# Layer 2's window attention: VectorE in a written order, the routing in set slots, the bias of the values and the experts' bias moved, the second norm from the first variance, the first expert weights asked for earlier

## The chip, the cores and the metric

The kernel runs on one core of a Trainium2 chip. The metric is the device time of one execution in microseconds. TensorE (PE) does the matmuls and transposes, VectorE (DVE), ScalarE (ACT) and GpSimd (POOL) the elementwise work, and SyncE (SP) issues most DMAs; each runs its own list of instructions in order and waits on semaphores for the others. All data are fp32.

## The reference

Four layers work on two images of 256 channels and 32 x 32 positions, that is 2048 tokens. Layers 0 and 1 are attentions over the images, layers 2 and 3 work on tokens. Layer 2, which the change touches:

```python
t = t + window_attention(layernorm(t))       # 8 heads of 32, windows of 64 tokens, shifted by 32
t = t + moe(layernorm(t))

def moe(x):                                  # 8 experts, two a token
    p = softmax(x @ Wr + br); top_p, top_i = top_k(p, 2); w = top_p / top_p.sum()
    xn = layernorm(x)                        # a second norm, on the norm's output
    y[e] = gelu((xn * ln_g[e] + ln_b[e]) @ W1[e] + b1[e]) @ W2[e] + b2[e]
    return sum(w[k] * y[top_i[k]] for k in range(2))
```

The window attention computes q, k and v from the normed tokens with a bias each, softmax(q k / sqrt(32) + relative position) v in each window, and a projection with the bias b_out. Layer 3 is an additive attention (tanh of all pairs of tokens in blocks of 1024) and another MoE.

## The kernel before, in words

Tokens are held as 16 tiles of 128 (`t`, 128 partitions x 16 x 256), eight tiles an image. Layers 0 and 1 take the span up to about 1640 us and are not touched. Then comes `window_attention` (L778), and at its end the generator of the routing is handed to `Late.run` (L1704), which plans the rest.

**The attention loop.** The first image is normed and transposed (`normed`, L824: 12 small VectorE instructions for the inverse root, 8 scales, 16 transposes, 4 copies). Six instructions or groups of them make one tile's way, spread over five rounds of a software pipeline (`for i in range(NT + 4)`): round i does `value(i)` (v, L898), `scores(i)` (q k, L871, then on VectorE L876 scale and bias, L882 maximum, L883 subtraction, on ScalarE L884 exp, on VectorE L885 sum and L886 reciprocal, on GpSimd L889 the two products that give the probabilities), `turn(i-2)` (transposes of the probabilities L908, copies L909 on ScalarE), a `project` of the next group of four tiles (q and k, L852, for the first 12 rounds), a step of the second image's `normed` (the first six rounds), `sums(i-3)` (L917, copy L925) and `output(i-4)` (L931; L935 adds b_out on VectorE into y; L936 adds y to t on GpSimd). From round 10 three pieces a round are taken of `late.dispatch(2, 0)`, the routing of the first image (in this code an image is a "b" of 8 tiles).

PE and ACT run the loop in the order in which it is written (`manual_schedule`); for DVE, POOL and SP a scheduler chooses the order.

**The routing (`Late.dispatch`, L1144).** For each half of four tiles, `gate` (L1127) norms the tokens (statistics L1087 and L1088, inverse root L1066 to L1079, scale L1097), transposes (L1108) and computes the router's logits (L1137). `route` (L1192) makes softmax, top two, the number of tokens of each expert, the slot of each token, the row of each weight tile and the shares. The second norm takes statistics of u again and scales it. Then 16 indirect DMAs on GpSimd (L1161, "the scatter") bring the tokens to their experts' slots in DRAM. At last `shift` (L1173) adds the experts' bias b2 to `t`, weighted by the shares: a transpose of the weights (ps_wT, L1179), matmuls (ps_b, L1187) and additions into `t`.

**The rest is planned by numbers.** In `Late.run` a dictionary gives each step a start and the distance of its pieces, in units of a made-up clock; `merge` interleaves the steps' pieces by it. D20 and D21 are the two images' dispatch, E20 and E21 the experts (each slot tile: xr read back by SP L1371, ps_x transposes L1379, ps_h L1404, gelu, ps_y L1424), C20 and C21 collect the results, A0 and A1 the additive attention (tanh L1622, ps_e L1631), and so on. Up to the start of E21 in the plan DVE, PE and ACT are scheduled, from there on they keep the written order. The experts' weights ("ew") are fetched tile by tile with indirect DMAs on GpSimd (L1322), into six buffers.

Of the kernel before, what the change touches and what calls it, by code (L numbers as in the profile page):

```python
# [19 lines left out]
F32 = mybir.dt.float32  # L20
I32 = mybir.dt.int32
U32 = mybir.dt.uint32
AF = mybir.ActivationFunctionType
# [4 lines left out]
P = 128  # L28
# [41 lines left out]
class Stack:  # L70
# [707 lines left out]
    def window_attention(self, t, late):  # L778
# [7 lines left out]
        with ExitStack() as ctx:  # L786
# [6 lines left out]
            w_qkv = self.load(w, "w_qkv", "(c p) o -> p c o", p=P)  # L793
            w_out = self.load(w, "wa_w_out", "(c p) o -> p c o", p=P)
            b_qk = self.load(w, "b_qk")
            b_v, b_out = self.load_row(w, "b_v"), self.load_row(w, "wa_b_out")


            rel = self.ins["rel_pos"]
# [19 lines left out]
            for x in probs:  # L819
                nc.gpsimd.memset(x, 0.0)  # L820

            uT, q, k, v, pT, o = {}, {}, {}, {}, {}, {}

            def normed(b):  # L824

# [19 lines left out]
            def project(g, part):  # L845

                if part == 0:
                    q[g], k[g] = (sb.tile([P, CC, CH], F32, name=n) for n in ("qh", "kh"))
                x, at = uT[g // 2], g % 2 * CH
                ps = late.misc([P, CH], "ps_qk")  # L850
                for c in range(CC):
                    nc.tensor.matmul(  # L852
                        ps, lhsT=w_qkv[:, c, part * P : (part + 1) * P], rhs=x[:, c, at : at + CH],
                        start=(c == 0), stop=(c == CC - 1),
                    )
                to = (q if part < CC else k)[g][:, part % CC, :]
                if part < CC:
                    nc.scalar.activation(to, ps, AF.Identity, bias=b_qk[:, part : part + 1])
                else:
                    nc.vector.tensor_scalar(to, ps, b_qk[:, part : part + 1], None, ALU.add)  # L860

            def scores(i):

                g, at = i // 4, (i % 4) * P
                s = p_s.tile([P, 4, CH], F32, name="ps_s")
                for o in range(CC):
                    for h in range(4):
                        rows = slice(D * h, D * (h + 1))
# [12 lines left out]
                m, rec = (self.small.tile([P, H], F32, name=f"wa_{n}") for n in ("m", "rec"))  # L881
                nc.vector.tensor_reduce(m, l, AX.X, ALU.max)  # L882
                nc.vector.tensor_tensor(l, l, broadcast(m, [P, H, WIN]), ALU.subtract)  # L883
                nc.scalar.activation(l, l, AF.Exp)  # L884
                nc.vector.tensor_reduce(m, l, AX.X, ALU.add)  # L885
                nc.vector.reciprocal(rec, m)  # L886
                for r in range(2):
                    rows = slice(WIN * r, WIN * (r + 1))
                    nc.gpsimd.tensor_tensor(  # L889
                        probs[i % RING][rows, :, rows], l[rows], broadcast(rec[rows], [WIN, H, WIN]), ALU.mult  # L890
                    )

            def value(i):
                x = uT[i // IT][:, :, i % IT * P : (i % IT + 1) * P]
                v[i] = sb.tile([P, C], F32, name="va", bufs=4)
                ps = late.misc([P, C], "ps_va")
                for c in range(CC):
                    nc.tensor.matmul(  # L898
                        ps, lhsT=x[:, c, :], rhs=w_qkv[:, c, 2 * C :], start=(c == 0), stop=(c == CC - 1)
                    )  # L900
                nc.vector.tensor_tensor(v[i], ps, b_v, ALU.add)

            def turn(i):
                pT[i] = sb.tile([P, H, P], F32, name="ptT")
# [22 lines left out]
            def output(i):  # L927
                x = o.pop(i)
                ps = late.misc([P, C], "ps_wo")
                for c in range(CC):  # L930
                    nc.tensor.matmul(  # L931
                        ps, lhsT=x[:, c, :], rhs=w_out[:, c, :], start=(c == 0), stop=(c == CC - 1)
                    )
                y = sb.tile([P, C], F32, name="y")
                nc.vector.tensor_tensor(y, ps, b_out, ALU.add)  # L935
                nc.gpsimd.tensor_tensor(t[:, i, :], t[:, i, :], y, ALU.add)  # L936

            for _ in normed(0):
                pass
            route, other = late.dispatch(2, 0), normed(1)  # L940
            engines = mybir.EngineType
            with tc.manual_schedule(engines={engines.PE, engines.Activation}):
                for part in range(2 * CC):
                    project(0, part)
                for i in range(NT + 4):
                    if i < NT:
                        value(i)
                        scores(i)
                    if 2 <= i < NT + 2:
                        turn(i - 2)  # L950
                    if i + 4 < NT:
                        project(i // 4 + 1, i % 4)
                    if i < 6:
                        next(other, None)
                    if 3 <= i < NT + 3:
                        sums(i - 3)
                    if 4 <= i:
                        output(i - 4)
                    if i >= 10:
                        for _ in range(3):  # L960
                            next(route, None)
            return route


# [25 lines left out]
class Late:  # L990
# [3 lines left out]
    def __init__(self, ctx, stack, t):  # L994
# [2 lines left out]
        nc, tc = self.nc, self.tc  # L997
        self.w = ctx.enter_context(tc.tile_pool(name="late_w", bufs=1))
        self.early = ctx.enter_context(tc.tile_pool(name="early_sb", bufs=2))
        self.made = {}  # L1000
        self.u, self.uT, self.logits, self.routes, self.affine, self.kT, self.qb = ({} for _ in range(7))

# [90 lines left out]
    def scale(self, dst, src, tiles, mv):  # L1093
        nc = self.nc
        rs = self.inverse_root(mv[:, :, 1], 1e-5)
        for k, i in enumerate(tiles):
            nc.vector.tensor_scalar(  # L1097
                dst(i), src(i), mv[:, k, 0:1], rs[:, k : k + 1], ALU.subtract, ALU.mult
            )
# [44 lines left out]
    def dispatch(self, *key, done=0):  # L1144

        l, b = key
        tokens = GROUPS[key]
        n = len(tokens)
        for half in range(done, n // 4):
            yield from self.gate(l, b, half)  # L1150
        yield from self.route(key, n)
        u = self.u[key]
        if l == 2:
            yield from self.norm(lambda i: u[:, i, :], lambda i: u[:, i, :], range(n))
        p, shares, slots, rows = self.routes[key]
        nc = self.nc

        before = []
        for i in range(n):
            for slot in slots:  # L1160
                ins = nc.gpsimd.indirect_dma_start(  # L1161
                    out=self.stack.slots_in[b % 2],
                    out_offset=bass.IndirectOffsetOnAxis(ap=slot[:, i : i + 1], axis=0),
                    in_=u[:, i, :], in_offset=None,
                ).ins
                for other in before:
                    self.tc.declare_no_dep(ins, other, reason="a slot takes one token")
                before.append(ins)
            yield None if l == 2 else 0.5
        if l == 2:  # L1170
            yield from self.shift(*key)

    def shift(self, *key):  # L1173

# [529 lines left out]
    def run(self, route):  # L1704
# [2 lines left out]
        self.sb = self.ctx.enter_context(self.tc.tile_pool(name="late_sb", bufs=2))  # L1707
        self.misc = lambda shape, name: p_m.tile(shape, F32, name=name, tag="ps_m")
        self.p_x, self.p_h, self.p_y, self.p_e = psum("lt_x", 1), psum("lt_h", 2), psum("lt_y", 1), psum("lt_e", 1)
        self.loaded = [  # L1710
            [self.sb.tile([P, WIDE], F32, name=f"ew{k}", bufs=LANES[2]) for k in range(2)] for _ in range(LANES[2])
        ]


        plan = {
            "D20": (route, (), -12, 0.86),
            "E20": (self.experts(2, 0, then=(2, 1)), ("D20",), 0, 2.4),
            "D21": (self.dispatch(2, 1), (), 5, 3.45),
            "E21": (self.experts(2, 1), ("D21", "E20"), 172, lambda now: 2.43 if now < 205 else 4.4),
            "C20": (self.collect(2, 0), ("E20",), 172, 2.0),  # L1720
            "A0": (self.additive(0), ("C20",), 211, 4.75),
            "N30": (self.gate(3, 0, 0), ("A0 half",), 420, 6.0),
            "C21": (self.collect(2, 1), ("E21",), 456, 2.0),
            "A1": (self.additive(1), ("C21", "A0 tanh"), 500, 4.6),
            "D30": (self.dispatch(3, 0, done=1), ("A0", "N30"), 515, 2.0),
            "E30": (self.experts(3, 0, then=(3, 1)), ("D30",), 600, 4.4),
# [110 lines left out]
```

## Time and profile before

| | us |
|---|---|
| median of 3 runs (lowest, highest) | 2885.95 (2885.02, 2887.11) |
| profiled execution | 2887.74 |
| its span, first to last instruction | 2886.0 |
| PE busy | 2635.3 (91%) |
| DVE, ACT, POOL busy | 1944.8, 1815.6, 1235.5 |
| mean granted clock of TensorE | 0.967 |
| first projection of layer 2 starts | 1640.51 |
| first scatter starts, last lands | 1779.64, 1803.88 |
| first expert matmul | 1810.59 |

The page gives busy time by engine, then the span in 40 slices with the busy share of each in tenths, the DMA queues, the chain of work that ended last, the costliest groups of instructions and the DMA issues. "Idle before" is idle time of an engine just ahead of an instruction, put down to what ended it. "L876" is a line of the kernel. In the order of time of one engine, a row has its start, its duration, the engine, the line, the operation, out<-in, and shapes as partitions x elements.

### The profile page before, as it was taken

The page shows a single profiled execution, that of the slowest core. Times are in us where ns is not written, and L with a number is a line of the kernel's source. Part 1 is how long each engine was busy: PE and PEld are TensorE (multiplying, and loading weights), DVE is VectorE, ACT ScalarE, POOL GpSimd, SP SyncE. Part 2 cuts the span into 40 slices and gives each one's busy share as a digit, 9 for nine tenths or more (in the row PEclk, how much of TensorE's full clock was granted, in tenths as well). Part 3 has the DMA queues.
Part 4 walks back from the last instruction along what each step waited for, and adds up shares of the span by engine and source line. Part 5 has one row for each costly group of instructions (what it writes and reads, how often), then busy time and mean ns, then how long its engine had stood idle before and what let it go on. Part 6 is the DMA issues. An engine that isn't in the chain of part 4 may idle for free. (4 is left out here: it accounts for less than half of the span.)

```text
span 2886.0 us, 77396 instructions
## 1 busy us (share of the span) xinstructions
PE 2635.3 (91%) x32006; PEld 1643.6 (57%) x32006; DVE 1944.8 (67%) x3642; ACT 1815.6 (63%) x2685; POOL 1235.5 (43%) x1302
## 2 busy tenths in 40 slices
PE   7899999999999998799999686999999988999987
PEld 3455555555555555555555454998666632465676
DVE  5999999999999999478789577633422343134242
ACT  2777777778777777255555231211699878889722
POOL 4877777777777775001111134244111112102242
PEclk9999999999999999899999897999999999899998
DMA  3000000000000000111010100543222001322354
GB/s 133 3 3 3 3 3 3 3 3 3 3 3 3 3 3 3 49 31 28 11 31 9 28 1 30 202 134 99 68 81 76 16 24 35 128 67 87 116 166 125
DMA packets 180577, 131.39 MB, mean 46 GB/s; under 512 B 130992, under 2 KB 162368, under 8 KB 173056
## 3 DMA queue, kind: packets, MB, share of 16 engines
q0 software_dynamic: 29232, 81.71, 8.5%
q1 hardware_dynamic: 147824, 44.25, 6.8%
q8 instruction: 251, 4.11, 0.6%
q10 hardware_dynamic: 3168, 0.48, 0.1%
q14 instruction: 102, 0.84, 0.1%
HBM read 181.24 MB, written 29.49 MB: 73 GB/s over the span
## 5 line engine op out<-in xcount | busy, mean ns | idle before, releaser
L188 ACT ACTIVATE sc<-sc,sa_shift 128x1024 f32<-128x1024 f32 x512 | 584.5, 1144 | 153.1 <-DMA sa_shift<-sa_min 150.8
L201 DVE STREAM_TRANSPOSE wt<-sc 128x1024 f32<-128x1024 f32 x512 | 601.5, 1207 | 0.2 <-ACT sc L188 0.2
L1622 ACT ACTIVATE th<-kT,qb 128x1024 f32<-128x1024 f32 x512 | 540.4, 1135 | 66.2 <-PE ps_e L1631 40.1
L211 PEld LDWEIGHTS ps_o<-wt,v 128*64 128x64 f32 x8192 | 444.4, 137 | 188.9 <-issue 106.2
L143 PE MATMUL ps_s<-kT,qT 64*32 64x512 f32 x8192 | 527.6, 595 | 18.0 <-ACT sc L153 17.2
L211 PE MATMUL ps_o<-wt,v 128*64 128x128 f32 x8192 | 505.0, 276 | 26.8 <-DVE oT L372 26.7
L166 POOL TENSOR_TENSOR fold<-sc 128x512 f32<-128x512 f32 x256 | 329.2, 1286 | 195.9 <-ACT sc L153 177.0
L168 POOL TENSOR_TENSOR fold<-sc,fold 128x512 f32<-128x512 f32 x256 | 328.4, 1283 | 21.4
L153 ACT COPY sc<-ps_s 128x1024 f32<-128x1024 f32 x256 | 256.0, 1000 | 111.0 <-PE ps_s L143 57.1
L1631 PE MATMUL ps_e<-th,pick 128*32 128x512 f32 x2048 | 305.7, 613 | 20.5 <-ACT th L1622 9.3
L1404 PEld LDWEIGHTS ps_h<-xe,ew 128*128 128x128 f32 x2320 | 278.1, 194 | 63.6 <-issue 39.0
L150 DVE TENSOR_SCALAR_CACHE_REDUCE sc<-ps_s 128x1024 f32<-128x1024 f32 x256 | 304.3, 1189 | 7.1 <-PE ps_s L143 6.6
L1404 PE MATMUL ps_h<-xe,ew 128*128 128x128 f32 x2320 | 295.0, 281 | 13.7 <-issue 5.6
L1424 PE MATMUL ps_y<-ew,h 128*128 128x256 f32 x1160 | 275.6, 387 | 8.2 <-ACT h L1410 5.6
L143 PEld LDWEIGHTS ps_s<-kT,qT 64*32 64x32 f32 x8192 | 134.4, 106 | 230.2 <-issue 163.4
L1424 PEld LDWEIGHTS ps_y<-ew,h 128*128 128x128 f32 x1160 | 215.6, 193 | 66.7 <-issue 23.0
L630 ACT ACTIVATE sc<-sc,l_least 128x1024 f32<-128x1024 f32 x128 | 146.7, 1147 | 125.8 <-DVE sc L617 125.5
L1415 DVE TENSOR_TENSOR hb<-ps_h,ew 128x512 f32<-128x512 f32 x115 | 79.4, 691 | 207.3 <-PE ps_h L1404 167.1
L1428 DVE COPY y<-ps_y 128x256 f32<-128x256 f32 x99 | 41.9, 423 | 229.7 <-PE ps_y L1424 209.9
L1393 ACT ACTIVATE h<-hb 128x512 f32<-128x512 f32 x115 | 71.5, 623 | 193.0 <-DVE hb L1415 173.7
L636 DVE STREAM_TRANSPOSE wt<-sc 128x1024 f32<-128x1024 f32 x128 | 153.3, 1225 | 46.0 <-ACT sc L630 25.4
L617 DVE TENSOR_SCALAR_CACHE_REDUCE sc<-ps_s 128x1024 f32<-128x1024 f32 x128 | 150.7, 1213 | 40.3 <-PE ps_s L609 40.2
(286 smaller groups left out, 3139.1 us busy)
## 6 DMA issues: line engine op xcount, KB each, us to landing
xr<-slots_in SPq DMA_DIRECT2D x99, 128.0 KB
slots_out<-y SPq DMA_DIRECT2D x99, 128.0 KB
sa_got<-sa_least SPq DMA_DIRECT2D x512, 0.5 KB
sa_shift<-sa_min SPq DMA_DIRECT2D x512, 0.2 KB
slots_in<-zero POOLq DMA_DIRECT2D x46, 128.0 KB
kh<-kh SPq DMA_DIRECT2D x32, 128.0 KB
qh<-qh SPq DMA_DIRECT2D x32, 128.0 KB
sa_sums<-sa_total SPq DMA_DIRECT2D x244, 1.0 KB
```

What stands on the lines that cost most here:

```text
L143: nc.tensor.matmul(ps[r][S * c : S * (c + 1), a, :].rearrange("p (b i) -> p b i", i=S), lhsT=qT[half, p, S * i : S * (i + 1)], rhs=keys[ha ...
L150: nc.vector.tensor_scalar(scores[m][0], flat[0], 1.0, None, ALU.mult, ALU.min, accum_out=least[m // 2][:, 0, h : h + 1])
L153: nc.scalar.copy(scores[m][1], flat[1])
L166: nc.gpsimd.tensor_tensor(y, a, b, ALU.subtract)
L168: nc.gpsimd.tensor_tensor(y, a, y, ALU.subtract)
L188: nc.scalar.activation(scores[m][r], scores[m][r], AF.Exp, bias=shift[m // 2][:, r : r + 1], scale=-1.0, accum_out=total[i][:, 2 * p + r, ...
L201: nc.vector.transpose(weights[i, h][:, 2 * p + r, :], x)
L211: nc.tensor.matmul(sums[i][64 * k : 64 * (k + 1)], lhsT=v[:, at % NT, 64 * (at // NT) : 64 * (at // NT + 1)], rhs=weights[i, h][:, :, S * ...
L1404: nc.tensor.matmul(ps[:, j, :], lhsT=a[:, c, at : at + P], rhs=x[:, c, :], start=(c == 0), stop=(c == CC - 1),)
L1424: nc.tensor.matmul(ps, lhsT=h[:, j, :], rhs=w2[:, j, :], start=(j == 0), stop=(j == HB - 1))
L1622: nc.scalar.activation(h, keys, AF.Tanh, bias=self.qb[b][:, s // G, g : g + 1])
L1631: nc.tensor.matmul(pe[i][c * U : (c + 1) * U, a, :], lhsT=self.pick[:, k, :], rhs=h[:, a, :], start=(k == 0), stop=(k == G - 1),)
```

## The change

Five parts, all of them in layer 2:

- VectorE joins PE and ACT in the written order of the loop, and the loop's body is cut differently for it: the softmax's sum, reciprocal and probabilities become `divide(i)`, after `sums(i-3)`. The 32 pieces of the routing are taken in numbers set round by round, half of them ahead of `output`, half behind.
- b_v no longer is added to the values. Since each row of probabilities sums to 1, it is put through the output projection once (`output_shift`, four matmuls with b_v spread over the columns) and added to b_out. b_out is added to `t` by GpSimd, tile by tile; `output` adds ps_wo to `t` on VectorE, in one instruction. The copies of v and the bias of k go to ScalarE.
- The variance after the first norm is var * rs * rs, so the second norm's statistics are not taken; its scaling goes to ScalarE, and the norm comes ahead of `route`. (The mean after the first norm is taken as zero.)
- `shift` leaves `dispatch` and becomes two steps of the plan, B20 at 100 and B21 at 215; C20 and C21 wait for them.
- The first expert weights (up and down of slot tile 0) are fetched before the scatter; the six weight buffers move to a pool that is there from the start.

```diff
-            b_v, b_out = self.load_row(w, "b_v"), self.load_row(w, "wa_b_out")
+            b_v, b_out = self.load(w, "b_v", "(c p) -> p c", p=P), self.load_row(w, "wa_b_out")
...
+            spread = w.tile([P, CC, P], F32, name="spread")
+            nc.gpsimd.tensor_copy(spread, broadcast(b_v, [P, CC, P]))
+
+            def output_shift():
+                ps = late.misc([P, C], "ps_wo")
+                for c in range(CC):
+                    nc.tensor.matmul(
+                        ps, lhsT=spread[:, c, :], rhs=w_out[:, c, :], start=(c == 0), stop=(c == CC - 1)
+                    )
+                nc.vector.tensor_tensor(b_out, b_out, ps, ALU.add)
...
-                if part < CC:
-                    nc.scalar.activation(to, ps, AF.Identity, bias=b_qk[:, part : part + 1])
-                else:
-                    nc.vector.tensor_scalar(to, ps, b_qk[:, part : part + 1], None, ALU.add)
+                nc.scalar.activation(to, ps, AF.Identity, bias=b_qk[:, part : part + 1])
...
                 nc.scalar.activation(l, l, AF.Exp)
+                weights[i] = l, m, rec
+
+            def divide(i):
+                l, m, rec = weights.pop(i)
                 nc.vector.tensor_reduce(m, l, AX.X, ALU.add)
...
-                nc.vector.tensor_tensor(v[i], ps, b_v, ALU.add)
+                nc.scalar.copy(v[i], ps)
...
-                y = sb.tile([P, C], F32, name="y")
-                nc.vector.tensor_tensor(y, ps, b_out, ALU.add)
-                nc.gpsimd.tensor_tensor(t[:, i, :], t[:, i, :], y, ALU.add)
+                nc.vector.tensor_tensor(t[:, i, :], t[:, i, :], ps, ALU.add)
...
-            with tc.manual_schedule(engines={engines.PE, engines.Activation}):
+            pieces = {8: 1, 9: 1, 10: 1, 11: 1, 12: 2, 13: 2, 14: 3, 15: 3, 16: 4, 17: 4, 18: 4, 19: 6}
+            with tc.manual_schedule(engines={engines.PE, engines.Activation, engines.DVE}):
                 for part in range(2 * CC):
                     project(0, part)
+                output_shift()
...
+                    if 2 <= i < NT + 2:
+                        nc.gpsimd.tensor_tensor(t[:, i - 2, :], t[:, i - 2, :], b_out, ALU.add)
                     if 3 <= i < NT + 3:
                         sums(i - 3)
+                    if i < NT:
+                        divide(i)
+                    for _ in range(pieces.get(i, 0) // 2):
+                        next(route, None)
                     if 4 <= i:
                         output(i - 4)
-                    if i >= 10:
-                        for _ in range(3):
-                            next(route, None)
+                    for _ in range((pieces.get(i, 0) + 1) // 2):
+                        next(route, None)
...
+            [self.w.tile([P, WIDE], F32, name=f"ew{run}{k}") for k in range(2)] for run in range(LANES[2])
...
         rs = self.inverse_root(mv[:, :, 1], 1e-5)
+        self.last_norm = mv, rs
...
+        again = self.early.tile([P, n], F32, name="again", bufs=1) if l == 2 else None
         for half in range(done, n // 4):
             yield from self.gate(l, b, half)
-        yield from self.route(key, n)
+            if l == 2:
+                mv, rs = self.last_norm
+                to = again[:, 4 * half : 4 * half + 4]
+                nc.vector.tensor_tensor(to, mv[:, :, 1], rs, ALU.mult)
+                nc.vector.tensor_tensor(to, to, rs, ALU.mult)
         u = self.u[key]
         if l == 2:
-            yield from self.norm(lambda i: u[:, i, :], lambda i: u[:, i, :], range(n))
+            rs = self.inverse_root(again, 1e-5)
+            yield 3.0
+            for i in range(n):
+                nc.scalar.activation(u[:, i, :], u[:, i, :], AF.Identity, scale=rs[:, i : i + 1])
+            yield 5.0
+        yield from self.route(key, n)
         p, shares, slots, rows = self.routes[key]
+        if key == (2, 0):
+            self.fetch(key, 0)
+            self.fetch(key, 0, 1)
...
-        if l == 2:
-            yield from self.shift(*key)
...
+            "B20": (self.shift(2, 0), ("D20",), 100, 5.0),
+            "B21": (self.shift(2, 1), ("D21",), 215, 6.0),
-            "C20": (self.collect(2, 0), ("E20",), 172, 2.0),
+            "C20": (self.collect(2, 0), ("E20", "B20"), 172, 2.0),
-            "C21": (self.collect(2, 1), ("E21",), 456, 2.0),
+            "C21": (self.collect(2, 1), ("E21", "B21"), 456, 2.0),
```

More of the change, by code (lines that the diff above doesn't have):

```diff
@@ L820, in window_attention @@
                 nc.gpsimd.memset(x, 0.0)
-            uT, q, k, v, pT, o = {}, {}, {}, {}, {}, {}
+            uT, q, k, v, pT, o, weights = {}, {}, {}, {}, {}, {}, {}
+            spread = w.tile([P, CC, P], F32, name="spread")
[7 more added lines that the diff above has]
+                nc.vector.tensor_tensor(b_out, b_out, ps, ALU.add)
             def normed(b):
@@ L999, in __init__ @@
         self.early = ctx.enter_context(tc.tile_pool(name="early_sb", bufs=2))
+        self.loaded = [
+            [self.w.tile([P, WIDE], F32, name=f"ew{run}{k}") for k in range(2)] for run in range(LANES[2])
+        ]
         self.made = {}
@@ L1148, in dispatch @@
         n = len(tokens)
+        nc = self.nc
+        again = self.early.tile([P, n], F32, name="again", bufs=1) if l == 2 else None
         for half in range(done, n // 4):
             yield from self.gate(l, b, half)
-        yield from self.route(key, n)
+            if l == 2:
[3 more added lines that the diff above has]
+                nc.vector.tensor_tensor(to, to, rs, ALU.mult)
         u = self.u[key]
         if l == 2:
-            yield from self.norm(lambda i: u[:, i, :], lambda i: u[:, i, :], range(n))
+            rs = self.inverse_root(again, 1e-5)
[4 more added lines that the diff above has]
+        yield from self.route(key, n)
         p, shares, slots, rows = self.routes[key]
-        nc = self.nc
+        if key == (2, 0):
+            self.fetch(key, 0)
+            self.fetch(key, 0, 1)
         before = []
@@ L1709, in run @@
         self.p_x, self.p_h, self.p_y, self.p_e = psum("lt_x", 1), psum("lt_h", 2), psum("lt_y", 1), psum("lt_e", 1)
-        self.loaded = [
-            [self.sb.tile([P, WIDE], F32, name=f"ew{k}", bufs=LANES[2]) for k in range(2)] for _ in range(LANES[2])
-        ]
         plan = {
```

## The prediction

> **What bounds the kernel now.** I read the rows of 40 slices first, then the stages in windows, then the chain and the waits of layer 2, then single engines in order of time. A slice is 72.15 us; layer 2's attention lies in slices 23 to 25.
>
> ```profile
> PE   7899999999999998799999686999999988999987
> DVE  5999999999999999478789577633422343134242
> POOL 4877777777777775001111134244111112102242
> ```
>
> TensorE is full nearly everywhere; it falls to 6 and 8 tenths just where VectorE and GpSimd rise. The windows show the same by stage: after the times come busy time of PE, weight load, DVE, ACT and POOL, then granted clock, DMA share and GB/s.
>
> ```profile
> 1680.00:1715.00 35.00, 26.66 (x298) 16.18 (x296) 26.00 (x65) 9.84 (x21) 11.25 (x12) 1.00 0.01 1
> 1752.00:1780.00 28.00, 18.73 (x203) 13.49 (x205) 26.06 (x98) 7.58 (x17) 8.80 (x10) 0.80 0.00 1
> 1780.00:1810.00 30.00, 15.68 (x76) 9.78 (x70) 13.68 (x58) 1.39 (x4) 23.90 (x26) 0.62 0.37 132
> 1810.00:1990.00 180.00, 179.66 (x1220) 167.12 (x1219) 84.27 (x248) 32.97 (x50) 62.11 (x62) 0.99 0.41 138
> 2045.00:2300.00 255.00, 254.91 (x1806) 164.66 (x1805) 67.77 (x151) 234.00 (x245) 30.90 (x31) 1.00 0.18 59
> ```
>
> So the attention loop (1650 to 1780) is bound by no single engine at first and by VectorE at its end (26.06 of 28), the scatter (1780 to 1810) by GpSimd, and the expert stages after it by TensorE. Up to the first expert matmul (ps_h, 1810.59) time saved in the loop counts in full, since what follows is serial: 16 scatters from 1779.64, the read-back xr issued at 1804.15, landed at 1808.64. The waits between 1640 and 1810 say what holds the loop:
>
> ```profile
> ACT l L884 <- DVE l L883: 59.8, 12, 6.7
> POOL probs L889 <- DVE wa_rec L886: 42.1, 6, 25.9
> DVE n_st L1087 <- POOL t L936: 11.3, 8, 3.4
> ```
>
> The last is the one on the path: VectorE's statistics wait 11.3 us in 8 waits for GpSimd's residual add, with the next softmax behind them. The starts of l (L876) give the period: 1650.76 for tile 0, 1679.94 for 5, 1702.93 for 8, 1735.97 for 12, 1771.75 for 15. Between 5 and 8 that is 7.66 us a tile, where TensorE's own pieces sum to 5.8 (value .96, scores .42, turn .95, project 1.88, sums .57, output .97).
>
> One resource more. VectorE's subtraction L883 takes 0.69 alone, and more beside GpSimd's probs:
>
> ```profile
> 1656.01 1.56 DVE L883 TENSOR_TENSOR l<-l,wa_m 128x512 f32<-128x512 f32 x1
> ...
> 1667.14 0.69 DVE L883 TENSOR_TENSOR l<-l,wa_m 128x512 f32<-128x512 f32 x1
> ```
>
> ```profile
> 1654.88 2.15 POOL L889 TENSOR_TENSOR probs<-l,wa_rec 64x512 f32<-64x512 f32 x2 [25.89 <-DVE wa_rec L886]
> ```
>
> The slow one begins with the second probs instruction (1656.0) and ends .54 after it (1657.03): it did its work when GpSimd was through. Maxima, bn_stats and reads from PSUM at such places keep their times. The scale into u (L1097) shows it too: four took 2.18 at 1741.61 against 1.45 alone (4 x .36).
>
> **The change part by part**, against the profiled execution (2887.74 us, span 2886.0, 1.7 around it; it lies 1.8 above the median 2885.95).
>
> 1. *Into the loop.* `output_shift` puts 4 matmuls of ps_wo's shape (.97) on TensorE between the projections and tile 0; with its start otherwise unmoved (it waits for w_qkv until 1640.51), l of tile 0 starts 1.0 later. b_v's load changes its queue and is used by nothing before that; I price it at nothing, since both loads are issued ahead of w_qkv's landing, and at some 2 us if it came after.
>
> 2. *The residual bias.* In the order as built, GpSimd's 16 adds of b_out (L936's shape, .73) don't stand in the loop's rounds: GpSimd is not in the hand-set order, and they are put in two blocks of 8, ahead of probs 0 and between probs 0 and probs 1. The second 8 each wait for VectorE's scale of the same tile for image 1, which stands in VectorE's order between the subtraction and the sum of tile 1. VectorE must finish 8 scales (2.9 alone), and each next scale meets the add that the last one released. Bounds: 0 if they pass each other, 8 x .73 = 5.8 if each waits; the first block can hold up the subtraction of tile 0 and some of the 12 small root instructions, 0 to 1.5; and tiles 2 to 4, in a chain of exp, turn, transposes and copies, up to 1.7 more. The row nearest is L1097's .73 lost under one GpSimd instruction, so I go towards the upper end: tile 5 starts 6 us later than now (1686), bounds 1.7 (with the 1.0 of part 1) and 10.
>
> The Trainium skill ("SBUF — State Buffer", "Who interferes with whom") has the rule: the pair of ports shared by VectorE and GpSimd is locked for a whole instruction, and the other engine fully blocks. It speaks against this change, and the L883 row agrees. The page excepts a VectorE instruction with one SBUF operand unless it is in a 2-port mode; L1097 has one tensor operand and was slow here. Under the rule the scales cost 5.8, under its exception 0.
>
> 3. *The loop, tiles 5 to 12.* kh's 8 bias adds (.75) and the 16 value copies (.42) go to ScalarE, which is busy 9.84 of 35 there: 12.6 us off VectorE, hidden on ScalarE, whose copies then lie ahead of exp by .4 each. The wait of L1087 on GpSimd goes, because the residual sum is VectorE's own (.42, in place of y). VectorE per tile: l .67, max .72, subtract .72, wait for exp .76, sum .69, reciprocal .2, residual .42 = 4.2. Late next is TensorE: 5.8 + .4 for what remains of waits = 6.2, so tiles 5 to 8 take 18.55 where they took 22.99. From tile 8 route pieces are added: four statistics pairs (.56) 6.4; root 2.4 and four scales 1.45 and 1.4 of stalls 9.45; two copies of uT with their transposes 6.75; router (1.69 on TensorE) 7.55: 30.15 for 33.04. Sum -7.3.
>
> 4. *Tiles 12 to 15.* The second norm loses 8 bn_stats and 8 aggregates (4.5) and 8 scales (4.1) on VectorE and gains four small instructions (.8); ScalarE does the scaling (hidden, 7.58 of 28 busy). VectorE in its written order: 4.2 + .4 + 2.2 + 2.4 + 1.45 + 1.3 of stalls = 11.97; 8.8 with two copies and the second router; 9.65 with the second root. 30.4 for 35.78: -5.4.
>
> 5. *Tile 15 to the first scatter.* Today the route is mixed into the loop's end and the scatter starts 7.9 after l of tile 15. In the new slots softmax and first choice come at round 15, the rest at 16: 45 small instructions at .20 = 9.0, tile 15's own 4.2, 3.6 of stalls = 16.8: +8.9.
>
> Parts 2 to 5: first scatter at 1779.64 + 6 - 7.3 - 5.4 + 8.9 = 1781.8, **+2.2** (bounds -2.1 and +6.2; a further -5 if the stalls of parts 3 to 5 vanish).
>
> 6. *Scatter to first matmul.* Five residual adds leave GpSimd's scatter (2.55) and two fetches enter it (2 x 1.31): 0. The fetches lie before scatters 7 on, so the weights come earlier, but xr lands last today and still does.
>
> 7. *Moved matmuls.* In the built order image 1's second 8 transposes (1.04) and two routers (2 x 1.69) come before ps_x, in time when TensorE is idle (15.68 of 30); now they are in the stage where it is busy 179.66 of 180: **-4.4**. `shift` for image 0 takes the place of image 1's there: 0 (its old place, at clock .5, was hidden). Image 1's (2 x (.5+1+1) = 5.0) goes among ps_e, with TensorE at 254.91 of 255 but ScalarE also at 234: 0 if ScalarE's tanh sets the end, 5 if TensorE does; I take **+3**, nearer to the row of the fuller engine. Table loads (1.28 at 1815.5 and 1846.17) are beside TensorE's work: 0.
>
> Sum +2.2 - 4.4 + 3 = +0.8: 2888.5 beside this execution, 2886.8 beside the median. I write **2886.5**.
>
> **Rivals.** Faster: adds and scales pass each other (part 2 at its lower bound, -2.1) and the stalls of 3 to 5 go too (-5): -7.1 - 4.4 + 3 = -8.5, 2877.5. For it: bn_stats and PSUM reads show no stall, and TensorE has 8 us of slack in 1680 to 1715 for making up lag. Against it: L883 and L1097.
>
> Slower: the written order of VectorE keeps the lag. Everything behind a held-up scale (sum and reciprocal of tile 1, so probs 1, its turn, image 1's uT) waits with it; tile 5 is then 10 late, image 1's shift is paid in full (+5), and transposes and routers run at the clock of .65 (a router took 3.15 there for 1.69), 1.5 of it on the path twice: +6.2 - 4.4 + 5 + 3 = +9.8, 2896. It decides from a lag of 9 us at tile 5. For it: clock .62 in 1780 to 1810, .80 before. Against it: TensorE's margin in tiles 5 to 8.
>
> The change doesn't do what it says: the loop is in VectorE's order, but the adds aren't in it; that is in the forecast already. If the period stays 7.66 because ScalarE's added work delays exp, part 3 loses its 4.4 in tiles 5 to 8: 2891, within the forecast's own range.
>
> **How the numbers follow.** No change (own range 2881 to 2892): .40; faster: .33; slower: .27. 0.2% is 5.8 us, about what can be told from no change. Two in ten cut off evenly from the outer cases leave 2875 to 2897.
>
> **What would show it.** Starts of l: tile 5 near 1686 (1682 for the faster case, 1690 for the slower); a period of 6.2 from 5 to 8; GpSimd's adds in two blocks with scales stretched to about 1.0; first scatter at 1782 and, as now, 31 us from it to the first ps_h; 4.4 less between the first ps_h and the last ps_y of image 0; the tanh stage 3 longer. It is wrong if the scales stay at .36, if the period stays above 7, or if later stages, whose plan is by numbers, fall differently.

## The result, and the profile after

The changed kernel is slower: 2897.45 us, median of 8 runs (2892.46 to 2902.53), against 2885.25 for the kernel before (8 runs, 2879.55 to 2888.22); ratio 1.0047, 95% interval 1.0036 to 1.0059. The forecast was no change at 2886.5, the range ended at 2897.0. The profiled execution took 2902.53 us, the slowest of the eight; its span is 2900.8, 14.8 more than the span before, where the medians differ by 12.2.

The same three rows of 40 slices, of the changed kernel:

```profile
PE   7899999999999998799999686899999989899987
DVE  5999999999999998377788456343522343134242
POOL 4877777778777775011111333244111011102142
```

In slices 23 to 26 VectorE reads 4 5 6 3 where it read 5 7 7 6, so work has left it; TensorE reads 6 8 6 8 for 6 8 6 9, so its hole has not closed. The stages tell more. In the lines of the changed kernel L885 is the scale and bias of l (before: L876), L898 the softmax's sum (L885), L947 the residual (L935), L970 GpSimd's add of b_out, L1132 the copies of uT (L1109) and L1160 the router (L1137). Windows of the kernel before and after, cut at tile 0, tile 8, tile 15 (starts of l), first scatter and first ps_h; columns as in the windows above. Before:

```profile
1702.93:1771.75 68.82, 49.26 (x510) 34.28 (x509) 55.58 (x175) 14.35 (x31) 19.67 (x21) 0.84 0.00 1
1779.64:1810.59 30.95, 16.62 (x82) 10.56 (x81) 14.63 (x61) 1.75 (x4) 24.73 (x26) 0.62 0.38 136
```

After:

```profile
1652.11:1707.68 55.57, 45.20 (x482) 27.60 (x482) 36.24 (x66) 20.66 (x43) 27.75 (x31) 0.91 0.01 1
1707.68:1773.57 65.89, 51.81 (x520) 36.90 (x518) 42.70 (x120) 18.42 (x40) 14.75 (x15) 0.82 0.01 1
1773.57:1791.66 18.09, 13.59 (x106) 9.95 (x104) 14.69 (x76) 8.12 (x20) 2.08 (x2) 0.72 0.00 1
1791.66:1827.21 35.55, 12.11 (x51) 10.48 (x51) 18.72 (x87) 2.41 (x7) 21.92 (x22) 0.54 0.62 228
```

Between tiles 8 and 15 VectorE's work fell by 12.9 us (55.58 to 42.70), as the prediction had it leave; the stage got only 2.9 shorter. VectorE now stands idle 23.2 us there, where it stood 13.2. Its waits in that window of the changed kernel (total, times, longest):

```profile
DVE l L885 <- PE ps_s L880: 6.9, 4, 2.1
DVE wa_m L898 <- ACT l L893: 5.3, 7, 0.8
DVE t L947 <- PE ps_wo L944: 4.9, 5, 1.7
DVE rt_lg L1164 <- PE ps_router L1160: 4.1, 2, 2.8
```

In the kernel before the first two are not in the list of that window at all. What stands behind such a wait, from VectorE in order of time:

```profile
1714.62 0.18 DVE L1110 BATCH_NORM_AGGREGATE n_mv<-n_st 128x2 f32<-128x6 f32 x1
...
1717.59 0.69 DVE L898 TENSOR_REDUCE wa_m<-l 128x8 f32<-128x512 f32 x1 [0.76 <-ACT l L893]
1718.31 0.20 DVE L899 RECIPROCAL wa_rec<-wa_m 128x8 f32<-128x8 f32 x1
1719.25 0.42 DVE L947 TENSOR_TENSOR t<-t,ps_wo 128x256 f32<-128x256 f32 x1 [0.74 <-PE ps_wo L944]
1719.59 0.16 DVE L1094 TENSOR_SCALAR ir_x<-n_mv 128x4 f32<-128x4 f32 x1
```

The routing's inverse root (from L1094 on) has its input n_mv at 1714.80 and starts at 1719.59, behind two waits of .75 in which VectorE does nothing. The time of each stretch in the profiled executions, with the prediction's terms:

| stretch | before | after | difference | predicted |
|---|---|---|---|---|
| span's start to tile 5 | 1679.94 | 1688.54 | +8.6 | +6 |
| tile 5 to 12 | 56.03 | 53.70 | -2.3 | -7.3 |
| tile 12 to 15 | 35.78 | 31.33 | -4.4 | -5.4 |
| tile 15 to first scatter | 7.89 | 18.09 | +10.2 | +8.9 |
| first scatter to first ps_h | 30.95 | 35.55 | +4.6 | 0 |
| first ps_h to first tanh | 238.6 | 233.2 | -5.4 | -4.4 |
| first tanh to the end | 836.8 | 840.4 | +3.6 | +3 |
| sum | | | +14.8 | +0.8 |

The two blocks of GpSimd's adds are where the built order had them:

```profile
1651.25 5.98 POOL L970 TENSOR_TENSOR t<-t,sb_wa_b_out 128x256 f32<-128x256 f32 x8 [8.32 <-DVE sb_wa_b_out L834]
1659.86 2.15 POOL L902 TENSOR_TENSOR probs<-l,wa_rec 64x512 f32<-64x512 f32 x2 [2.63 <-DVE wa_rec L899]
1663.03 5.84 POOL L970 TENSOR_TENSOR t<-t,sb_wa_b_out 128x256 f32<-128x256 f32 x8 [1.02 <-DVE u L844]
```

And VectorE beside them:

```profile
1655.24 0.65 DVE L1095 TENSOR_SCALAR ir_half<-ir_x 128x8 int32<-128x8 int32 x1
...
1657.49 0.17 DVE L1101 SCALAR_TENSOR_TENSOR ir_y<-ir_a,ir_y 128x8 f32<-128x8 f32 x1
...
1662.49 5.11 DVE L844 TENSOR_SCALAR u<-t,tok_mv,ir_y 128x256 f32<-128x256 f32 x8
```

Four root instructions of .17 took about .65 until the first block ended at 1657.23, and the eight scales took 5.11 for 2.9. The last thing to see is the hand-over to the experts:

```profile
1808.88 0.16 DVE L1181 TENSOR_TENSOR again<-again,ir_y 128x4 f32<-128x4 f32 x1
...
1816.38 0.69 DVE L1132 COPY uT<-ps_tr 128x512 f32<-128x512 f32 x1 [7.35 <-remote]
...
1818.55 3.15 PE L1160 MATMUL ps_router<-sb_wr,uT 128*128 128x8 f32 x14 [0.82 <-DVE uT L1132]
...
1821.55 0.67 PE L1415 MATMUL ps_x<-ident,xr 128*128 128x128 f32 x2
1822.82 0.19 DVE L1164 TENSOR_TENSOR rt_lg<-ps_router,sb_br 128x32 f32<-128x32 f32 x1 [3.75 <-PE ps_x L1415]
...
1826.74 0.73 DVE L1419 TENSOR_SCALAR xe<-ps_x,rt_affine 128x128 f32<-128x128 f32 x2
1827.21 3.14 PE L1440 MATMUL ps_h<-xe,ew 128*128 128x128 f32 x13 [4.99 <-DVE xe L1419]
```

ps_x is through at 1822.2, but xe stands behind the second image's top two on VectorE, which waited for the router, which waited for a copy: 5.7 us from ps_x to ps_h where it was 1.5.

### The profile page after: what moved, and what is told of

It reads as the page before. It is cut to its first block, busy times and chain, and to the rows that moved or that the text cites. A ratio compares the mean times of both kernels' runs of the same rounds, so it can differ in the third digit from the quotient of the medians.

```text
span 2900.8 us, 77381 instructions
## 1 busy us (share of the span) xinstructions
PE 2646.8 (91%) x32010; PEld 1654.6 (57%) x32010; DVE 1927.4 (66%) x3579; ACT 1832.7 (63%) x2723; POOL 1236.6 (43%) x1303
## 5 line engine op out<-in xcount | busy, mean ns | idle before, releaser
L188 ACT ACTIVATE sc<-sc,sa_shift 128x1024 f32<-128x1024 f32 x512 | 585.0, 1145 | 155.9 <-DMA sa_shift<-sa_min 155.8
L1440 PE MATMUL ps_h<-xe,ew 128*128 128x128 f32 x2320 | 295.8, 281 | 20.2 <-DVE xe L1423 7.8
L1460 PEld LDWEIGHTS ps_y<-ew,h 128*128 128x128 f32 x1160 | 216.8, 194 | 64.6 <-issue 20.9
```

The lines of the kernel that those rows point to most:

```text
L188: nc.scalar.activation(scores[m][r], scores[m][r], AF.Exp, bias=shift[m // 2][:, r : r + 1], scale=-1.0, accum_out=total[i][:, 2 * p + r, ...
L1440: nc.tensor.matmul(ps[:, j, :], lhsT=a[:, c, at : at + P], rhs=x[:, c, :], start=(c == 0), stop=(c == CC - 1),)
L1460: nc.tensor.matmul(ps, lhsT=h[:, j, :], rhs=w2[:, j, :], start=(j == 0), stop=(j == HB - 1))
```

## The experiments

Ratios are to the kernel before on the same chip, with 95% intervals. Times between stages are counted from tile 0's l, since that start moves by some 5 us between these profiles. Each of the five groups (e1 to e4, e5 to e8, e9 to e12, e13 to e16, e17 and e18) ran on a chip of its own. On three of these the kernel before takes 2881 to 2887 us, on the chips of e9 to e12 and of e17 and e18 2847 to 2848; there the stretches behind the first ps_h are shorter for every kernel profiled. So only ratios are compared between groups, and these not finely: the changed kernel has 1.0047 in the result and 1.0068 in e14, one other program 1.0006 in e10 and .9991 in e15. Differences under some 2 thousandths (6 us) are read within a group alone.

**The adds: e1 and e2.** The first leaves out the bias of the attention's output.

```diff
-                    if 2 <= i < NT + 2:
-                        nc.gpsimd.tensor_tensor(t[:, i - 2, :], t[:, i - 2, :], b_out, ALU.add)
```

> The changed kernel without GpSimd's 16 adds of b_out to t (so the attention's output bias is left out of the result). Theory A, the adds: they hold up VectorE's root, scales and the first softmaxes, and all of the 8.6 us by which tile 5 is late come from them and from the 1 us of output_shift; without them tile 5 starts at about 1682, the first scatter at 1784 and the time is about 2890 (ratio to the kernel before 1.002). Theory B, VectorE's written order: tile 5 comes early, but the rounds from 8 on, where route pieces stand between the softmax steps, give it back; first scatter 1788 or later, time 2894 to 2897. Theory C, the second image's routing ahead of the first xe: the distance from ps_x to the first ps_h stays at 5.7 us in either case.

Ratio 1.0042 (1.0028 to 1.0056), 2893.8 us. Tile 5 at 32.1 us after tile 0 (after 36.4, before 29.2), first scatter at 133.7 (139.6, 128.9). So the adds cost 4.3 at tile 5 and 5.8 at the scatter in these profiles: more than half of tile 5's lag of 7.2 is theirs. How much of it the time keeps lies between nothing (1.0047 in the result) and 7.5 us (2901.3 for e3 below, on the same chip, which reaches the first ps_h as late as the changed kernel, 175.1 us after tile 0). The greater part of the slowdown is there without the adds.

e2 also puts back the old residual (y on VectorE, t + y on GpSimd).

> The changed kernel with the residual as before (VectorE adds b_out to ps_wo into y, GpSimd adds y to t); all else as changed. Theory A: the block of adds is gone, so tile 5 at 1682; but statistics wait again for GpSimd's add (.73 plus .2) in rounds 6 to 14; first scatter 1786 to 1790, time about 2893. Theory B: first scatter at 1790 or later, time 2896 to 2900, since VectorE's order with the new wait is worse.

Ratio 1.0043 (1.0027 to 1.0059), 2897.1 us. Tile 5 at 32.5, first scatter at 138.0. It is not the wait for GpSimd's add that makes the difference to e1: between tiles 5 and 15 none is in VectorE's list of waits, and behind tile 15 there is one, of .5 us. First scatter to ps_h takes 32.7, and the long wait of the uT copy isn't there.

**The second image's start: e3.** `"D21": (..., 5, 3.45)` becomes `25`.

> The changed kernel with the second image's dispatch planned at 25 where it was 5, so that the first xe no longer stands behind its routing in VectorE's order. Theory C: ps_x to first ps_h is 1.5 us for 5.7, but the transposes and routers (4.4) are again in the expert stage, where TensorE is full: net -4.1 + 4.4, about 2897 to 2898. If instead the 4.1 was not on the path, the time rises to about 2901. Theories A and B expect nothing of it.

Ratio 1.0071 (1.0054 to 1.0088). ps_x to first ps_h still takes 6.0: up to the start of E21 the scheduler orders TensorE and VectorE, and it moved the second image's ready work ahead of the waiting experts all the same. The edit didn't make the difference it was meant to make; it says nothing for or against theory C.

**VectorE's order: e4, e5, e6.** e4 takes VectorE out of the written order of the loop.

```diff
-            with tc.manual_schedule(engines={engines.PE, engines.Activation, engines.DVE}):
+            with tc.manual_schedule(engines={engines.PE, engines.Activation}):
```

> The changed kernel with VectorE out of the written order of the loop (the scheduler orders it, as before); GpSimd's order as built then has all 16 adds ahead of the first probabilities. Theory B: rounds 8 to 15 get faster, from 65.9 us between tiles 8 and 15 to about 60, and the first scatter comes within 10 us of tile 15 for 18; time about 2888 in spite of the adds. Theory A: the probabilities of tile 0 start 3 us later still (11.7 us of adds ahead of them), and time is 2898 to 2902.

Ratio 1.0004 (0.9994 to 1.0013), 2884.8 us: nearly the whole loss is gone, with all 16 adds in a block ahead of the first probabilities. Tiles 8 to 15 take 51.2 us (after 65.9, before 68.8). Its window from tile 8 to 15:

```profile
1706.78:1757.99 51.21, 44.14 (x506) 31.54 (x505) 37.85 (x108) 18.54 (x41) 13.08 (x13) 0.90 0.01 2
```

and VectorE's waits in it:

```profile
DVE rt_lg L1164 <- PE ps_router L1160: 4.1, 2, 2.8
DVE t L947 <- PE ps_wo L944: 3.8, 5, 0.9
DVE wa_m L898 <- ACT l L893: 2.3, 3, 0.8
DVE l L885 <- PE ps_s L880: 1.7, 3, 0.8
```

Idle time is 13.4 us, 23.2 in the written order. The window also holds 4.9 us less of VectorE's work, which comes behind tile 15: from there to the first scatter e4 takes 21.1 us for 18.1. In tiles 8 to 12 the work is the same (20.8 and 20.9 us), and there e4 takes 27.8 us for 34.6. The idle time fell where the written order had VectorE stand at the next instruction of its list: before the sum until exp is back (5.3 to 2.3), and before the next l until TensorE has scored (6.9 to 1.7). The route's small instructions that could have filled these holes stood behind.

TensorE's clock has a part in it. In tiles 8 to 12 its granted clock is .87 in the changed kernel and 1.00 in e4, and its work there takes 29.2 and 25.0 us (297 and 295 matmuls). In the changed kernel TensorE idles for 3.6 us from 1723.8 to 1727.4; in the 3 us from 1728.68 on the clock is .50, and tile 11's value and scores take 2.6 us (1730.94 to 1733.51) where tile 10's took 1.45. The same loop in e9 and e1 has a clock of .95 there and takes 32.4 and 32.6 us. So 4.6 us of the 6.8 between the two orders are there at nearly the full clock, and some 2 come with the low one. No run here holds the clock and changes the order alone.

The next two have the written order in rounds 0 to 7 only, and from round 8 on only; the loop is cut in two with one list of engines each.

> The changed kernel with VectorE in the written order only in rounds 0 to 7 and free from round 8 on, where the route pieces stand. Theory B1 (the order hurts where route pieces are cut into it): about the time of the kernel with a free VectorE, 2884 to 2887, tiles 8 to 15 in about 52 us and the first scatter about 129 us after tile 0. Theory B2 (it hurts from the first round): 2894 to 2897.

> The changed kernel with VectorE free in rounds 0 to 7 and in the written order from round 8 on. Theory B1: 2895 to 2899, tiles 8 to 15 in about 66 us. Theory B2: about 2886.

Ratios 1.0020 (1.0010 to 1.0031) and 1.0058 (1.0041 to 1.0075). Tiles 8 to 15 take 51.9 and 65.9 us, just as in the free and the written kernel, whatever came before them. Theory B1: the order hurts from round 8 on, where route pieces are cut into it. Between tiles 5 and 8, where none are, the written order takes 19.1 us and the free one 20.2. e5's ratio is not quite e4's, but the intervals overlap.

**The slots: e8.** Three pieces a round from round 10 on, as before, in the written order.

> The changed kernel with three route pieces a round from round 10 on, as before, VectorE in the written order. Theory D (the slots alone are wrong): 2888 to 2890, since the pieces end at round 19 with 30 taken and the second scales come earlier or later by at most a round. Theory B1 (any route piece in a written order costs the wait of the softmax beside it): 2895 to 2900.

Ratio 1.0054 (1.0037 to 1.0071). Tiles 8 to 12 take 38.7 us for 34.6, tile 15 to the first scatter 13.2 for 18.1; the scatter comes 5.9 sooner (133.6 after tile 0), but from it to the first ps_h it takes 38.8 for 35.6. The time is that of the changed kernel, as theory B1 has it: the set slots alone are not what slows it.

**The adds with a free VectorE: e7.** b_out goes into ps_wo by a matmul:

```diff
+                nc.tensor.matmul(ps, lhsT=late.ones[0:1, :], rhs=b_out[0:1, :], start=False, stop=True)
```

> The changed kernel with VectorE free and GpSimd's 16 adds taken out: b_out goes into ps_wo by a matmul of one row of ones with the row of b_out (16 more matmuls of 1 x 128 by 1 x 256). Theory A for what is left of the lag: tile 5 comes 31 us after tile 0 where it came 34.8 with a free VectorE and 36.4 in the changed kernel, and the time falls by about 4 to 2880 or 2881. If the adds don't matter once VectorE is free: 2885.

Ratio 1.0022 (1.0012 to 1.0032). Tile 5 comes at 29.7, the lag is gone as expected; the first scatter comes at 126.1 (e4 127.3), since the 16 more matmuls make the rounds longer (each has two rows in the trace, .69 us together; tiles 5 to 8 take 22.2 for 20.2). No gain.

**The hand-over: e9 and e10.** The plan's first part keeps the written order on TensorE and ScalarE, and the second image's dispatch starts at -30, so that its counts and its top two come behind the first experts. Both edits are in one run.

```diff
-        merge(plan["E21"][2])
         engines = mybir.EngineType
+        with self.tc.manual_schedule(engines={engines.PE, engines.Activation}):
+            merge(plan["E21"][2])
...
-            "D21": (self.dispatch(2, 1), (), 5, 3.45),
+            "D21": (self.dispatch(2, 1), (), -30, 3.45),
```

> The changed kernel with the first part of the plan in the written order on TensorE and ScalarE and the second image's dispatch planned from -30 on, so that its counts stand behind the first experts on TensorE and its top two behind the first xe on VectorE. Theory C: the first scatter to the first ps_h takes 31 to 32 us for 35.6, the first scatter stays at 140 us after tile 0, the time falls by about 4, ratio 1.003. If the lost 4 us come back in the expert stage (the routing that was in front has to go somewhere): ratio 1.0045 to 1.005.

> The changed kernel with VectorE free in the loop and the hand-over of the run before. If both causes are separate and add: first scatter 127 us after tile 0, first ps_h 31 to 32 us later for 38.4, time 6 below the kernel with a free VectorE alone, ratio 0.998. If the expert stage gives back what the hand-over gains: ratio 1.000.

The mechanism is as theory C has it: first scatter to ps_h 30.9 and 31.2 us for 35.6 and 38.4. The ratios don't show it: 1.0044 (1.0027 to 1.0062) and 1.0006 (0.9996 to 1.0015), while e10's first ps_h is at 155.9, 3.9 before that of the kernel before. But 4 us are 1.4 thousandths, less than the ratio of one program moves from chip to chip. What the time keeps of the 4.6 is not shown; in e10 there is no gain on the kernel before.

**Parts alone: e11 and e12**, in the kernel before.

> The kernel before with the second norm from the first variance alone (8 statistics, 8 aggregates and 8 scales off VectorE, four small instructions added, scaling on ScalarE); the norm stays behind the route. By part 4 of the prediction 7.8 us of VectorE's work go in a stage that it bounds: if that holds with a free order, the first scatter comes 4 to 8 us earlier and the time is 2878 to 2881 (ratio 0.998). If the scatter waits for the route's slots and not for u, nothing: 1.000.

> The kernel before with the experts' bias as two steps of the plan alone. By part 7: image 0's in the place of image 1's, image 1's 5.0 us of matmuls in the tanh stage, 0 to 5 of it on the path; ratio 1.000 to 1.002. If the emptier time before the first ps_x is filled with the second image's transposes and routers, 4.4 us come off the expert stage and the ratio is 0.9985 to 1.000.

The second norm alone: 1.0008 (0.9998 to 1.0018). Tile 15 comes 2.5 us earlier (118.5 for 121.0), the first scatter not (128.8). It doesn't wait for the route's slots, as the expectation's second case had it: these are there at 1777.8. ScalarE begins to scale u only at 1778.42, behind its copies, and GpSimd's residual add ends at 1779.41; the scatter starts at 1779.58. So the number came out by another wait. The bias as steps of the plan alone: 1.0016 (1.0005 to 1.0026), first ps_h at 159.1, so whatever it costs lies behind.

**Where the earlier start goes: e13 to e18.** First the kernels before and after once more, with e10's kernel and its variant with b_out on TensorE, on one chip.

> The kernel before once more, with a profile from the chip of the three runs beside it, so that stages can be set side by side. Ratio 1.000 within .001; tile 0 to the first ps_h 159 to 161 us.

> The changed kernel once more, for the stages on the same chip. Ratio 1.004 to 1.005; tile 0 to the first ps_h 174 to 176; the wait of the second uT copy of image 1 for about 7 us during the scatter is there again if it belongs to the program and not to one execution.

> The kernel with a free VectorE and the new hand-over again: first ps_h 155 to 157 us after tile 0, 4 before the kernel before. Theory E (the expert stage is bound by TensorE and takes what was taken out of it at the front): ps_h to the first tanh is 3 to 5 us longer than in the kernel before. Theory F (the tanh stage and what follows lose it, by the moved bias of image 1): first tanh to the end is 3 to 5 us longer. Ratio 1.000.

> The kernel with a free VectorE, the new hand-over, and b_out by a matmul of one row instead of GpSimd's adds. Tile 5 at 30 us after tile 0 for 33 to 35, first ps_h at 153 us. If the start of the experts counts in full: ratio 0.998 to 0.999; under theory E or F 1.000 or more.

Ratios 0.9998 (0.9989 to 1.0008), 1.0068 (1.0052 to 1.0085), 0.9991 (0.9979 to 1.0003), 1.0000 (0.9990 to 1.0010). Stages of these four profiles, in us:

| | e13 | e14 | e15 | e16 |
|---|---|---|---|---|
| tile 0 to first ps_h | 159.6 | 175.7 | 158.6 | 158.8 |
| first ps_h to first tanh | 238.6 | 233.5 | 235.3 | 235.1 |
| first tanh to the end | 840.5 | 842.4 | 844.3 | 844.4 |

The expert stage is 3 to 5 shorter, against theory E; the rest 2 to 4 longer, as theory F has it, but that stretch took 836.8 to 840.5 in two profiles of the kernel before. Two more kernels look at that: e17 is e10's with `shift` back in `dispatch` (B20 and B21 out of the plan), e18 has the old residual as well.

> The kernel with a free VectorE and the new hand-over, with the experts' bias back in the dispatch, as in the kernel before; image 0's lies ahead of the first experts, image 1's in the expert stage. Theory F (image 1's bias in the tanh stage costs its 4 to 5 us): first tanh to the end about 4 us shorter than with the bias in the plan, ratio 0.997 to 0.998. Theory E (the 5 us count in whichever full stage they lie): expert stage 0 to 1 longer, ratio as before, 0.999 to 1.000.

> As the run before, and the residual as in the kernel before (y on VectorE, added to t on GpSimd) in place of GpSimd's adds of b_out. Tile 5 at 30 us after tile 0, but GpSimd's adds lie among the scatters again (2.5 us). If the early lag counts: 2 to 3 us below the run before, ratio 0.995 to 0.997; if the scatter takes it back: equal.

e17: 0.9978 (0.9969 to 0.9987), 2841.3 us against 2847.9, the only version whose interval lies below 1. e18: 0.9999 (0.9990 to 1.0008); its first scatter comes at 129.8, 5.0 later than e17's, because VectorE's statistics wait for GpSimd's adds again (6.8 us in five waits between tiles 5 and 12, none in e17; tiles 8 to 12 take 32.5 us for 27.8). First and last tanh of e10, then of e17, whose spans are 2842.0 and 2834.1 (shortest, median and longest duration in ns, then first and last start):

```profile
L1658 ACT ACTIVATE th<-kT,qb x512: 1130/1133/1153, 2027.1 to 2678.3; 128x1024 f32<-128x1024 f32 x171
```

```profile
L1660 ACT ACTIVATE th<-kT,qb x512: 1128/1133/1156, 2025.6 to 2671.4; 128x1024 f32<-128x1024 f32 x171
```

Both start the tanh stage 377.8 to 377.9 us after tile 0; from there to the end e10 takes 814.9 and e17 808.5. TensorE's busy time in that stretch is 763.3 and 757.3, with 24 matmuls more in e10: those of image 1's bias, whose 16 ps_b of .374 lie at 2041.5 to 2078.0 in e10 and in the expert stage (1897.4 to 1918.9) in e17. In e17 image 0's bias is back in the time before the first ps_x, when TensorE is idle, and the first ps_h comes no later for it (156.0 for 155.9). But e10 and e17 ran on two chips. e12 and e11, on one chip, differ by the same 24 matmuls in that stretch and take 811.7 and 810.7 us. So these profiles agree with theory F in the sign, and the size lies between 1.0 and 6.4 us; what else e17's gain is made of stays open.

Within one chip the largest step is e14 to e15: a free VectorE and the new hand-over take the changed kernel from 2905.6 to 2885.0 us.

## Why the prediction was wrong

By its own steps, against the table of stretches:

- **Part 3 failed**, "30.15 for 33.04" for tiles 8 to 12: 34.56 was measured (32.4 to 34.6 in the runs with this order and these slots). The single instructions were right (root 2.4, four scales 1.38 for 1.45), and tiles 5 to 8 took 19.14 for 18.55. What was missing is that in a written order the waits add up in both directions: VectorE stands for exp and for ps_wo, TensorE then stands for VectorE, and its next scores come late (6.9 us of waits for ps_s in tiles 8 to 15, none before). The sum had one wait a tile, for exp, and TensorE's 5.8 a tile at the full clock, where .87 was granted. e4 to e6 show it: the same work in a free order takes 27.78.
- **Part 6 failed**, "Five residual adds leave GpSimd's scatter (2.55) and two fetches enter it (2 x 1.31): 0": +4.6. It looked at the scatter and xr and not at what lies ahead of the first xe in VectorE's list, though part 7 had just moved the second image's routing there. e9, with another order there, has 30.9. The count in the text is off too: four residual adds, not five, stand between the scatters of the kernel before; the 2.55 holds.
- **Part 7** came close by these two profiles: -5.4 for -4.4, and +3.6 for +3 from the first tanh to the end. The second is no test of its size: two profiles of the kernel before differ by 3.7 there, e11 and e12 put the bias of image 1 at 1.0, e10 and e17 at 6.4. Part 7 had said itself that image 0's old place was hidden, and did not draw from it that moving the bias could only lose.
- **Part 2** was mis-sized by 2.6 (8.6 for 6): the scales lost 2.2 instead of up to 5.8, the root and the subtraction 2.3, tile 0 itself came 1.35 later, and about 3 came without the adds (e1: 32.1 after tile 0 for 29.2), in the written order of rounds 1 to 5.
- **Parts 4 and 5** held within 1.3 each: -4.4 for -5.4, +10.2 for +8.9.

The rival on the slower side, at 2896, came closest, in part by luck. Its mechanism held in two points: the lag stayed (8.6, just short of the 9 from which it was to decide), and the routers at the hand-over ran at 3.15 under a granted clock of .54. That image 1's bias was paid in full is not shown. A bigger share, the waits from round 8 on, it did not have. Of the adds: by the rule of the Trainium skill ("SBUF — State Buffer", "Who interferes with whom") that the other engine is blocked for a whole instruction, the scales would lose 8 x .73 = 5.8, an estimate, if the shared ports are taken. The profile shows 2.2: eight scales and eight adds, 2.9 and 5.84 us, are through in 6.4 (1662.49 to 1668.87), so the two streams run beside each other for part of the time.

What e17 keeps of the change is the residual on VectorE, b_v through the projection, ScalarE's copies and the second norm; what it drops is VectorE's written order and the moved bias, and it has the new hand-over besides. The early fetch is in every version of the changed kernel and was not tried alone; nor was a written order for GpSimd, which would have put the adds into their rounds.

## What to carry to other kernels

An engine's work that goes is time only if what stands next in its list can run: VectorE lost 12.9 us of work between tiles 8 and 15 and gained 10 us of waits, because a written order puts independent small work behind a wait that it could have filled. Here the holes that this left in TensorE's work cost a second time, since its granted clock was lower behind them (.87 for 1.00 in tiles 8 to 12). Before moving work, ask whether its old place cost anything: one image's bias lay in idle time of TensorE and was moved into a full stage. A program's ratio can differ by 2 thousandths between chips, so a small gain is read beside its rival on one chip. And where two stages meet, read the in-order list of every engine that feeds the first instruction of the next, not only the transfer that lands last.

## What was not expected of the hardware

In the changed kernel, in e1 and in e3 VectorE's copy of the second image's transposes starts 5.7 to 6.5 us after TensorE's last recorded transpose, 1.0 to 1.7 us after the last scatter's instruction has ended (in e14 3.7 and .5 us); VectorE is idle for 7.35, 6.6 and 6.4 us before it, and the profile names no releaser in this program ("remote"). In e2 and e9 the same copy starts at once. What holds it was not found.

With a free VectorE (e4, e5) dependent small instructions of the second image's routing ran at a pitch of 1.4 us just behind the last scatter (in e4 from 1802.4 on, with weight fetches until 1807.5), each waiting 1.2 us for VectorE's own instruction before it. From e4, VectorE in order of time:

```profile
1805.91 0.23 DVE L1254 TENSOR_TENSOR rt_eq<-rt_lg,rt_one 128x64 f32<-128x64 f32 x1 [1.18 <-DVE rt_one L1253]
1807.31 0.23 DVE L1255 TENSOR_TENSOR rt_eq<-rt_eq,rank 128x64 f32<-128x64 f32 x1 [1.17 <-DVE rt_eq L1254]
1808.71 0.22 DVE L1256 TENSOR_REDUCE rt_one<-rt_eq 128x8 f32<-128x64 f32 x1 [1.17 <-DVE rt_eq L1255]
```

Elsewhere such a pair is .2 to .26 apart. The waits begin in GpSimd's stretch of indirect DMAs and are not in e10 or e15, where this work comes later; the cause was not tried.
